# Moving the norms' transposes, and a row-wise Hadamard transform, from TensorE to GpSimd, VectorE and DRAM in an adaLN block

## The chip, the cores and the metric

The kernel runs on one core of a Trainium2 chip. The metric is the device time of one execution in microseconds; lower is better. The core has TensorE (PE in the profile; its weight loads are PEld), VectorE (DVE), ScalarE (ACT), GpSimd (POOL) and SyncE (SP), which here only issues transfers. TensorE writes to PSUM, which has eight banks in this kernel; everything else lives in SBUF, 128 partitions wide, or in DRAM.

## The reference, cut to what matters

The input x is 4 sequences of 1024 tokens by 512 channels, all in float32. Each sequence has its own modulation vectors, from which the norms' scales (ca, cb), shifts (sa, sb) and gates (ga, gb) come.

```python
h = layernorm(x) * (1 + ca) + sa
x = x + ga * attention(h)            # 16 query heads of 32, one shared key/value head, causal
h = layernorm(x) * (1 + cb) + sb
x = x + gb * ffn(h)

def ffn(h):
    x = fwht(h * SU_ug) / 64         # Hadamard transform over the 512 channels
    up, gate = (x @ W_up.T) * .., (x @ W_gate.T) * ..
    x = fwht(silu(gate) * up * SU_dp) / 64
    return (x @ W_down.T) * ..
```

What the change touches: the first norm's output h is needed with channels on the partitions (transposed), since the query, key and value products contract over channels. The second norm's output is needed transformed by fwht and transposed in the same way, since the up and gate products contract over channels too. The second fwht is not touched: it is folded into W_down at the start.

## The kernel before, in words

The 4096 tokens are worked off in eight blocks of 512 tokens, in the order `order` (sequence and half of the sequence: (0,0), (1,0), (0,1), (2,0), (1,1), (2,1), (3,0), (3,1)). A block has four tiles of 128 tokens, and two halves of 256 tokens. In the code `i` counts blocks from 0, `hh` counts halves over all blocks (0 to 15), `n` counts tiles over all blocks (0 to 31).

The work is written as streams (Python generators). Each stream yields operations (`Op`) with an engine, a planned cost, and the keys that it reads and writes. A planner (`Flow`) takes, again and again, the operation that can begin first by its planned times, with the streams' ranks to choose among those that begin within 0.3 us, and emits it. So the order of instructions on each engine, and of transfers on the SP queue, is fixed when the program is built; on the chip each engine works through its own order and waits wherever an input is late. All loads and stores of this change go through one queue, SP's (`load`, one issue line for all of them).

The streams that matter here:

- `first_norms`: for each half, loads two tiles (xn), takes statistics on VectorE (`stats_op`), the reciprocal root on GpSimd (`rstd_op`), normalizes on VectorE (`norm_op`), turns the half by eight TensorE transposes of 128x128 into two PSUM banks (`turned`, L315), and ScalarE applies scale and shift on the way into hT (`modulate`, L324).
- `fronts`: the key/value and query products from hT (L289). hT is a single buffer of one half, so the next half's hT waits for these products.
- `scores`, `minima`, `exps`, `reciprocals`, `scales`, `turns`, `attend`, `finish`: attention for each tile of 128 queries, ending in the output projection (L289, `ow`) and the multiplication by the gate on VectorE (L644).
- `add`: reloads the tile of x (xr, two slots), adds the output bias and the attention's result on GpSimd (L659, L661), stores the sum, and normalizes it (statistics L294, rstd L300 and L301, L305).
- `second_norms`: for each half, eight transposes (L315), ScalarE modulation into u2 (L324), one butterfly over pairs of 128-channel chunks on GpSimd (VectorE in the first block) into v4 (L689, L692), four Hadamard products by a 128x128 matrix (L700), a copy on ScalarE (L705) and two butterfly steps on VectorE (L708) into bt. Then four differences (L712) prepare Strassen-like sums of the activations. bt holds one block, so bt is refilled only after the block before has finished its gate and up products (`st.gated`).
- `gate_up`: the gate and up products by a seven-product scheme (L982) with 16 steps of 128 hidden channels per block; weights wg (two slots) and wu (three slots) are loaded per step, and GpSimd forms sums of them (`mixes`, L946). Partial results are summed on VectorE (L1069) and copied by ScalarE (L1056, L1060); `multiply` applies silu (L1085 to L1095).
- `down`: W_down products (L1120): 16 steps for the first half of the block (beside the gating) and 16 for the second half (after it), with one load of wd (three slots) per step.
- `outputs`: multiplies by the gate gb (L1149), adds x on GpSimd (L1154), and stores.

`gate_up` and `down` have the lowest ranks: TensorE does attention and norms first and fills up with feed-forward work.

Of the kernel before, what the change touches and what calls it, by code (L numbers as in the profile page):

```python
# [19 lines left out]
P = 128  # L20
# [3 lines left out]
NT = TB // P  # L24
# [136 lines left out]
def adaln_block(ctx, tc, x_d, small_d, const_d, wmod_d, qwT_d, kwT_d, vwT_d, vb_d, owT_d, ob_d,  # L161
# [5 lines left out]
    dram = ctx.enter_context(tc.tile_pool(name="dram", bufs=1, space=DRAM))  # L167
    psum = ctx.enter_context(tc.tile_pool(name="psum", bufs=1, space=PSUM))
    flow, banks = Flow(), Banks()
    ps = psum.tile([P, 8, 512], F32, name="ps")  # L170

    def sb(name, *shape):
# [1 line left out]

    x2_d = dram.tile([B * S, D], F32, name="x2_d")
    wd_d = dram.tile([NFC, P, D], F32, name="wd_d")
    gates_d = dram.tile([3, B, D], F32, name="gates_d")
    rows = [slice(HD * j, HD * j + HD) for j in range(4)]


# [51 lines left out]
    ga, obga, y = sb("ga", D), sb("obga", D), sb("y", D)  # L232

    u2, v4 = sb("u2", 2, HB), sb("v4", NDC, HB)

    make_identity(nc, ident)
    nc.gpsimd.memset(mhalf, -0.5)
# [66 lines left out]
    def norm_op(x, xk, m, rs, rkey):  # L304
        return Op("DVE", 0.62, lambda: nc.vector.tensor_scalar(x, x, m, rs, ALU.subtract, ALU.mult), [rkey], [xk])  # L305

    def turned(x, xk, done=None):

        yield banks.have(2)
        bb = banks.take(2)  # L310

        def turns():
            for dc in range(NDC):
                for j in range(2):
                    nc.tensor.transpose(ps[:, bb[dc // 2], (dc % 2) * HB + j * P:][:, 0:P],  # L315
                                        x[:, j, dc * P:(dc + 1) * P], ident)
        yield Op("PE", 8 * 0.107 + 0.05, turns, [(xk, 0), (xk, 1)], [bk(b) for b in bb], mode="full")
        found.append(bb)
# [10 lines left out]
    def first_norms(halves):  # L329
        for hh in halves:  # L330
            i, hf = divmod(hh, 2)
            b = order[i][0]

            x, xk = (xo, "xo") if hh == 1 else (xn, "xn")
            yield lambda: st.fronts >= (hh - 1 if hh > 1 else 0)
            for j in range(2):
                r = token(2 * hh + j)
                yield load(0.25, x[:, j, :], x_d[r:r + P, :], [(xk, j)])
            m = mv["a"][:, hf]
            for j in range(2):  # L340
                yield stats_op("a", j, x[:, j, :], m[:, j, :], [(xk, j)], ("mva", hf, j))
            rs = rstd["a"][:, hf, :]
            yield rstd_op(rs, m[:, :, 1], [("mva", hf, 0), ("mva", hf, 1)], ("rstda", hf))
            for j in range(2):
                yield norm_op(x[:, j, :], (xk, j), m[:, j, 0:1], rs[:, j:j + 1], ("rstda", hf))
            yield lambda: st.fronts >= hh
            yield from turned(x, xk)
            bb = found.popleft()
            for dc in range(NDC):
                yield modulate(hT[:, dc, :], bb, dc, modT[:, 1, dc, b:b + 1], modT[:, 0, dc, b:b + 1],  # L350
                               ["mod0", "mod1"], [("hT", dc // 2 * 2)])
                if dc % 2:
                    banks.give(bb[dc // 2])
            st.first_normed = hh + 1
# [294 lines left out]
    def add():  # L649

        for i in range(NBLK):
            if new_batch(i):
                yield load(0.25, obga, gates_d[2, order[i][0], :].partition_broadcast(P), ["obga"], [("gates", 2)])
            for ql in range(NT):
                j, n = ql % 2, i * NT + ql
                x, xk, r = xr[:, j, :], ("xr", j), n * P
                yield lambda: st.turned > n - 2
                yield load(0.25, x, x_d[token(n):token(n) + P, :], [xk])
                yield Op("POOL", 1.3, lambda: nc.gpsimd.tensor_add(x, x, obga), ["obga"], [xk])  # L659
                yield lambda: bool(to_add)  # L660
                yield Op("POOL", 1.3, lambda: nc.gpsimd.tensor_add(x, x, y), ["y"], [xk])  # L661
                to_add.popleft()
                st.y_held = False
                yield load(0.25, x2_d[r:r + P, :], x, [("x2", n)], [xk])
                m, rs = mv["f"][:, j, :], rstd["f"][:, j, 0:1]
                yield stats_op("f", n, x, m, [xk], ("mvf", j))
                yield rstd_op(rs, m[:, 1:2], [("mvf", j)], ("rstdf", j))
                yield norm_op(x, xk, m[:, 0:1], rs, ("rstdf", j))
                st.added = n + 1

    def second_norms():


        for i in range(NBLK):
            b = order[i][0]
            for hf in range(2):
                n0 = i * NT + 2 * hf
                yield lambda: st.added >= n0 + 2
                yield from turned(xr, "xr")
                bb = found.popleft()  # L680
                st.turned = n0 + 2
                for c in (0, 2):
                    for dc in (c, c + 1):
                        yield modulate(u2[:, dc - c, :], bb, dc, sc2[:, dc, b:b + 1], bi2[:, dc, b:b + 1],
                                       ["mod4"], ["u2"])
                    banks.give(bb[c // 2])
                    for e, dc in (("add", c), ("sub", c + 1)):
                        if i:
                            yield Op("POOL", 0.66, lambda: getattr(nc.gpsimd, "tensor_" + e)(  # L689
                                v4[:, dc, :], u2[:, 0, :], u2[:, 1, :]), ["u2"], [("v4", dc)])  # L690
                        else:
                            yield Op("DVE", 0.4, lambda: getattr(nc.vector, "tensor_" + e)(  # L692
                                v4[:, dc, :], u2[:, 0, :], u2[:, 1, :]), ["u2"], [("v4", dc)])
                yield lambda: st.gated >= i
                yield banks.have(2)
                bb = banks.take(2)

                def products():
                    for dc in range(NDC):
                        nc.tensor.matmul(ps[:, bb[dc // 2], (dc % 2) * HB:][:, 0:HB], had, v4[:, dc, :],  # L700
                                         start=True, stop=True)
                yield Op("PE", mm(HB, 4), products, [("v4", dc) for dc in range(NDC)] + ["had"],
                         [bk(b) for b in bb], mode="full")
                w2 = u2.rearrange("p a n -> p (a n)")
                yield Op("ACT", act_cost(512), lambda: nc.scalar.copy(w2, ps[:, bb[1], :]), [bk(bb[1])], ["u2"])  # L705
                banks.give(bb[1])
                for e, k in (("add", hf), ("sub", 2 + hf)):
                    yield Op("DVE", 0.7, lambda: getattr(nc.vector, "tensor_" + e)(  # L708
                        bt[:, k].rearrange("p a n -> p (a n)"), ps[:, bb[0], :], w2), [bk(bb[0]), "u2"], [("bt", k)])
                banks.give(bb[0])  # L710
            for o, u, w in ((T1, B12, B11), (T2, B22, T1), (T3, B22, B12), (T4, B21, T2)):
                yield Op("DVE", 0.7, lambda: nc.vector.tensor_sub(bt[:, o], bt[:, u], bt[:, w]),  # L712
                         [("bt", u), ("bt", w)], [("bt", o)])
            st.normed = i + 1
# [60 lines left out]
    def mods():  # L775
        for _ in range(6):
# [42 lines left out]
            if part == 4:  # L819
# [5 lines left out]
                        nc.vector.tensor_scalar_mul(sc2[:, dc, :], modT[:, 3, dc, :], sus[:, dc:dc + 1])  # L825
                        nc.vector.tensor_scalar_mul(bi2[:, dc, :], modT[:, 2, dc, :], sus[:, dc:dc + 1])
                yield Op("DVE", 1.0, scales, ["mod3"], ["mod4"])
            if part in (2, 5):
                for g in ((0, 2), (), (), (1,))[part - 2]:
                    v = gt[:, g, 2]  # L830
                    yield banks.have(1)
                    o, = banks.take(1)

                    def turn_back():
                        for dc in range(NDC):
                            nc.tensor.matmul(ps[0:B, o, dc * P:(dc + 1) * P], v[:, dc, :], ident, start=True, stop=True)
# [322 lines left out]
    def early(rank, later):  # L1159
# [1 line left out]

    ranked = [
        (0, copies), (0, sums), (0.5, multiply), (1, outputs), (0.2, load_weights_once), (2, load_jobs), (2, mods),
        (early(1.8, 3), attend), (early(1.8, 3), finish), (early(1.8, 3), add), (early(2.2, 4), minima), (early(2.05, 4), scores), (early(1.7, 5), second_norms), (0, lambda: first_norms([0])), (0.1, lambda: first_norms([1])), (2.1, lambda: fronts([0])),
        (6.1, lambda: first_norms(range(2, NHALF))),
        (6, lambda: fronts(range(1, NBLK))), (early(2.3, 7), turns), (early(2.5, 8), exps), (1.5, reciprocals), (early(2.4, 7.5), scales), (2.6, butterflies),
        (2.15, transforms), (0.3, mixes), (9, hand_over), (10, lambda: load_gu("wu", 3, wupT_d)), (10, lambda: load_gu("wg", 2, wgT_d)), (10, load_wd),
# [54 lines left out]
```

## Time and profile before

| what | value |
|---|---|
| median of 3 runs | 2108.74 us (2106.20 to 2109.54) |
| profiled execution | 2106.39 us, its span 2104.6 us |
| granted TensorE clock, mean | 0.992 |
| TensorE busy | 2029.8 us |
| VectorE busy | 1325.7 us |
| ScalarE busy | 1174.0 us |
| GpSimd busy | 663.4 us |
| transposes of the norms (L315) | 256 instructions |
| Hadamard products of the second norm (L700) | 128 instructions |
| DMA engines busy, queue of SP | 31.4% |

How to read the profile: a line of the cost groups names the source line, the engine, the operation, output and input tiles, their shapes and the count; then, after the bar, busy time in us and the mean of one in ns; then the engine's idle time just before these instructions and what ended it. The chain of work that ended last is followed back from the last instruction; its pieces show what set the time. A float32 product counts as two TensorE instructions, a transpose as one. A transfer's "us to landing" runs from its issue to the arrival of its data.

### The profile page before, as it was taken

How to read it: one execution, taken by the hardware profiler on the slowest of the kernel's cores; microseconds unless marked ns; L12 is line 12 of the kernel's file. 1: busy time of each engine (PE TensorE's matmuls, PEld its weight loads, DVE VectorE, ACT ScalarE, POOL GpSimd, SP SyncE). 2: the span in 40 equal slices, each digit the busy share in tenths (PEclk: the TensorE clock that was granted, in tenths of full speed). 3: DMA queues.
4: the chain of work that ended last, by engine and by line, in shares of the span. 5: the costliest groups of instructions: out<-in, count | busy, mean ns of one | idle time of the engine just before them, and what ended most of it. 6: DMA issues, size and time to landing. Idle time of an engine off the chain costs nothing.

```text
span 2104.6 us, 41766 instructions
## 1 busy us (share of the span) xinstructions
PE 2029.8 (96%) x16408; PEld 1306.5 (62%) x16408; DVE 1325.7 (63%) x3085; ACT 1174.0 (56%) x2497; POOL 663.4 (32%) x814
## 2 busy tenths in 40 slices
PE   6989999999999999999999999999999999999998
PEld 4457666566656666646667476665666646675774
DVE  3975657776864657576874676784755878542441
ACT  3856746665744756465663676567744667431220
POOL 2572342223331242323331133231432223232331
PEclk9889999999999999999999999999999999999999
DMA  6144222432233322342221432232322233225333
GB/s 207 57 131 131 81 86 76 121 106 72 76 91 91 116 85 72 86 136 86 81 76 57 132 90 85 62 91 86 110 76 66 71 112 91 78 86 148 110 101 115
DMA packets 222075, 201.54 MB, mean 96 GB/s; under 512 B 14252, under 2 KB 161836, under 8 KB 221880
## 3 DMA queue, kind: packets, MB, share of 16 engines
q1 hardware_dynamic: 217944, 196.45, 31.4%
q8 instruction: 129, 2.11, 0.4%
q10 hardware_dynamic: 3936, 2.43, 0.4%
q14 instruction: 66, 0.54, 0.1%
HBM read 177.84 MB, written 21.00 MB: 94 GB/s over the span
## 4 chain that ended last, share of the span: by engine, by line
PE 89%; DVE 5%; issue 2%; DMA 1%; POOL 1%; ACT 1%; SPq 0%; ACTq 0%; POOLq 0%; DVEq 0%
PE ps L982 37%; PE ps L1120 20%; PE ps L289 12%; PE ps L591 9%; PE ps L467 7%; DVE p L563 2%; PE ps L627 2%; DVE p L491 1%; PE ps L315 1%; PE ps L700 1%; DMA raw<-in_wmod 1%; DVE g L1095 1%; DVE s L1069 0%; POOL p L545 0%; PE ps L890 0%
## 5 line engine op out<-in xcount | busy, mean ns | idle before, releaser
L1120 PE MATMUL ps<-wd,g 128*128 128x512 f32 x1024 | 479.7, 603 | 14.1 <-DVE g L1095 11.3
L514 ACT ACTIVATE p<-p,nm 128x512 f32<-128x512 f32 (+7 forms) x512 | 391.3, 768 | 29.0 <-DVE nm L491 28.8
L982 PE MATMUL ps<-bt,ws 128*128 128x256 f32 x1536 | 376.5, 381 | 1.3 <-ACT s L1056 1.3
L548 ACT ACTIVATE p<-p,rden 128x640 f32<-128x640 f32 (+7 forms) x480 | 349.7, 784 | 42.9 <-DVE rden L528 42.2
L1069 DVE TENSOR_TENSOR s<-ps,s 128x256 f32<-128x256 f32 x384 | 160.2, 420 | 330.4 <-PE ps L982 250.8
L563 DVE STREAM_TRANSPOSE p<-p 128x512 f32<-128x512 f32 (+7 forms) x256 | 340.8, 1358 | 27.7 <-ACT p L548 24.5
L1120 PEld LDWEIGHTS ps<-wd,g 128*128 128x128 f32 x1024 | 185.0, 189 | 232.8 <-issue 180.0
L982 PEld LDWEIGHTS ps<-bt,ws 128*128 128x128 f32 x1536 | 288.9, 190 | 60.5 <-issue 13.4
L491 DVE CUSTOM_DVE_ANT_0 p<-ps,maskw 128x512 f32<-128x512 f32 (+3 forms) x512 | 276.9, 582 | 75.5 <-PE ps L467 75.0
L946 POOL TENSOR_TENSOR ws<-wu 128x256 f32<-128x256 f32 x128 | 105.3, 822 | 581.3 <-DMA wu<-in_wupT 556.9
L982 PE MATMUL ps<-bt,wu 128*128 128x256 f32 x1024 | 270.7, 387 | 0.5 <-DVE s L1069 0.5
L982 PE MATMUL ps<-bt,wg 128*128 128x256 f32 x1024 | 251.7, 382 | 1.3 <-DVE nm L491 0.6
L982 PEld LDWEIGHTS ps<-bt,wu 128*128 128x128 f32 x1024 | 187.7, 190 | 92.4 <-issue 53.4
L982 PEld LDWEIGHTS ps<-bt,wg 128*128 128x128 f32 x1024 | 192.0, 190 | 60.3 <-issue 26.2
L591 PE MATMUL ps<-p,vrep 32*32 32x256 f32 (+1 forms) x8256 | 198.1, 417 | 18.5 <-issue 9.2
L1085 ACT ACTIVATE th<-s,wgh 128x512 f32<-128x512 f32 x128 | 92.3, 721 | 182.3 <-DVE g L1095 122.5
L1060 ACT COPY s<-ps 128x256 f32<-128x256 f32 x128 | 47.5, 371 | 239.5 <-PE ps L982 238.9
L467 PE MATMUL ps<-kT,qT 32*128 32x512 f32 (+3 forms) x1536 | 178.7, 528 | 0.5 <-issue 0.2
L591 PEld LDWEIGHTS ps<-p,vrep 32*32 32x32 f32 x8256 | 121.4, 104 | 92.3 <-issue 35.3
L946 POOL TENSOR_TENSOR ws<-ws,wg 128x256 f32<-128x256 f32 x128 | 97.2, 760 | 173.6 <-DMA wg<-in_wgT 154.9
L604 ACT COPY oT<-ps 128x256 f32<-128x256 f32 x256 | 78.4, 383 | 126.7 <-PE ps L591 119.8
L491 DVE CUSTOM_DVE_ANT_0 p<-ps,maskw,nm 128x128 f32<-128x128 f32 (+3 forms) x256 | 127.9, 544 | 17.8 <-PE ps L467 17.6
(106 smaller groups left out, 2125.1 us busy)
## 6 DMA issues: line engine op xcount, KB each, us to landing
wd<-wd_d SPq DMA_DIRECT2D x256, 256.0 KB, 2.6
wu<-in_wupT SPq DMA_DIRECT2D x128, 256.0 KB, 2.8
wg<-in_wgT SPq DMA_DIRECT2D x128, 256.0 KB, 3.2
xr<-in_x SPq DMA_DIRECT2D x32, 256.0 KB, 3.1
x_d<-xr SPq DMA_DIRECT2D x32, 256.0 KB, 2.0
xo<-x_d SPq DMA_DIRECT2D x32, 256.0 KB, 3.9
out<-xo SPq DMA_DIRECT2D x32, 256.0 KB, 2.2
xn<-in_x SPq DMA_DIRECT2D x30, 256.0 KB, 3.3
```

The costliest lines, as they stand in the source:

```text
L289: nc.tensor.matmul(out, l, r, start=(k == 0), stop=(k == len(pairs) - 1))
L467: nc.tensor.matmul(ps[:, bb[j], m * n:(m + 1) * n], qT[r, c, u.ql * P:(u.ql + 1) * P], kT[r, u.kv[kb] * TB:u.kv[kb] * TB + n], start=True, ...
L491: yield Op("DVE", 0.245 + 0.00103 * n, lambda: nc.vector.tensor_tensor_reduce(o, ps[:, bb[j], k * n:(k + 1) * n], m, -1.0, nm[:, slot, 0, ...
L514: yield Op("ACT", act_cost(u.kmax) + 0.19, lambda: nc.scalar.activation(e, e, AF.Exp, bias=nm[:, slot, u.t, j:j + 1], scale=-1.0, accum_ou ...
L548: yield Op("ACT", act_cost(u.kmax), lambda: nc.scalar.activation(e, e, AF.Copy, scale=r), [("rden", ds, c)], [u.key(h)])
L563: yield Op("DVE", 0.135 + 0.00105 * 2 * u.kmax, lambda: nc.vector.transpose(e, e), [], [u.key(h), u.key(h + 1)])
L591: nc.tensor.matmul(ps[rows[c], bb[g], 0:w], vrep[rows[g], v0 + c, :], pv[rows[g], :, k:k + 32], start=(kt == 0), stop=(kt == nkt - 1))
L946: yield Op("POOL", 0.66, lambda: getattr(nc.gpsimd, "tensor_" + e)(a[o][0], a[x][0], a[y][0]), [a[n][1] for n in (x, y) if n != "A21" or o ...
L982: nc.tensor.matmul(o, w[:, c, :], bt[:, t, c, :], start=start and c == 0, stop=stop and c == 1, skip_group_check=True)
L1069: yield Op("DVE", 0.43, lambda: nc.vector.tensor_add(s[:, j, :], ps[:, bank, half * HB:(half + 1) * HB], s[:, j, :]), [bk(bank)], [sk[j]])
L1085: yield Op("ACT", act_cost(512), lambda: nc.scalar.activation(th, s[:, 0:2, :], AF.Tanh, scale=wgh[:, f:f + 1]), [sk[0], sk[1]], ["th"])
L1120: nc.tensor.matmul(ps[:, acc[j], :], g[:, j * P:(j + 1) * P], ff["wd"][:, m % NWD, :], start=(f == 0), stop=(f == NFC - 1))
```

## The change

Two constants, `ROWS, VIA_DRAM = 3, 4`, set from where the new way is used.

First norm, from half 4 (the third block) on: the normalized tile is transposed on VectorE, which turns each 32x32 square within the 128x512 tile in place. `turn` then stores the tile to DRAM (xT_d) with four transfers, one for each group of 32 partitions, which put the squares into their transposed places in runs of 32 elements (128 bytes). `turned_back` loads the transposed half from there into hT with two transfers, and ScalarE applies scale and shift in place in hT. The TensorE transposes of these halves and their PSUM banks go.

Second norm, from block 3 (the fourth) on: a new stream `transformed` applies scale and shift along the rows. Since channels now lie along the free axis, scale and shift are needed as rows, broadcast over the partitions; they are made at the start by two more turn-backs on TensorE, stored in gates_d, and loaded per sequence into v4's memory (sc2r, bi2r). VectorE does it in two scalar_tensor_tensor operations, which take the place of the normalization. GpSimd does the 512-point transform in nine steps, each an addition and a subtraction of even and odd elements (18 instructions of 128x256, back and forth between xr and ht, which lies in u2's memory). VectorE transposes the result, `turn` stores it, and `second_norms` loads it back into bt with two transfers per half. The transposes, the modulation, the butterflies and the Hadamard products of these blocks go; the four differences (L712) stay.

```diff
+    ROWS, VIA_DRAM = 3, 4
-    gates_d = dram.tile([3, B, D], F32, name="gates_d")
+    gates_d = dram.tile([5, B, D], F32, name="gates_d")
+    xT_d = {"a": dram.tile([NHALF, D, HB], F32, name="xTa_d"), "f": dram.tile([NHALF, D, HB], F32, name="xTf_d")}
...
+    ht = u2.rearrange("p a n -> p (a n)")
+    sc2r, bi2r = (v4[:, k:k + 2, :].rearrange("p a n -> p (a n)") for k in (0, 2))
...
+    def turn(which, n, x, xk):
+        hh, j = divmod(n, 2)
+        dst = xT_d[which][hh].rearrange("(b q) (j a i) -> j a q b i", q=32, j=2, a=4)[j]
+        for a, r in enumerate(rows):
+            yield load(0.0625, dst[a], x[r, :].rearrange("q (b i) -> q b i", i=32), [("xT", which, n, a)], [xk])
+
+    def turned_back(which, hh, c, dst, key):
+        return load(0.25, dst, xT_d[which][hh][c * P:(c + 2) * P, :].rearrange("(c p) n -> p c n", p=P), [key],
+                    [("xT", which, n, a) for n in (2 * hh, 2 * hh + 1) for a in range(4)])
...
@@ first_norms @@
+                if hh >= VIA_DRAM:
+                    yield Op("DVE", 0.67, lambda: nc.vector.transpose(x[:, j, :], x[:, j, :]), [], [(xk, j)])
+                    yield from turn("a", 2 * hh + j, x[:, j, :], (xk, j))
             yield lambda: st.fronts >= hh
+            if hh >= VIA_DRAM:
+                for c in (0, 2):
+                    yield turned_back("a", hh, c, hT[:, c:c + 2, :], ("hT", c))
+                for dc in range(NDC):
+                    yield Op("ACT", act_cost(HB), lambda: nc.scalar.activation(
+                        hT[:, dc, :], hT[:, dc, :], AF.Identity, bias=modT[:, 0, dc, b:b + 1],
+                        scale=modT[:, 1, dc, b:b + 1]), ["mod0", "mod1"], [("hT", dc // 2 * 2)])
+                st.first_normed = hh + 1
+                continue
...
@@ add @@
+                if i >= ROWS:
+                    to_fwht.append((n, m, rs))
+                    continue
...
+    def transformed():
+        for n in range(ROWS * NT, NBLK * NT):
...
+            yield lambda: bool(to_fwht)
+            _, m, rs = to_fwht.popleft()
+            yield Op("DVE", 0.7, lambda: nc.vector.scalar_tensor_tensor(x, x, m[:, 0:1], sc2r, ALU.subtract, ALU.mult),
+                     [("v4", 0), ("mvf", j)], [xk])
+            yield Op("DVE", 0.7, lambda: nc.vector.scalar_tensor_tensor(x, x, rs, bi2r, ALU.mult, ALU.add),
+                     [("v4", 2), ("rstdf", j)], [xk])
+            u, w = x, ht
+            for _ in range(9):
+                pairs = u.rearrange("p (n two) -> p two n", two=2)
+                for fn, h in (("add", 0), ("sub", D // 2)):
+                    yield Op("POOL", 0.66, lambda: getattr(nc.gpsimd, "tensor_" + fn)(
+                        w[:, h:h + D // 2], pairs[:, 0, :], pairs[:, 1, :]), [], [xk, "u2"])
+                u, w = w, u
+            yield Op("DVE", 0.67, lambda: nc.vector.transpose(x, ht), ["u2"], [xk])
+            yield from turn("f", n, x, xk)
+            st.added = st.turned = n + 1
...
@@ second_norms @@
+                if i >= ROWS:
+                    yield lambda: st.gated >= i
+                    for c in (0, 2):
+                        yield turned_back("f", 2 * i + hf, c, bt[:, c + hf], ("bt", c + hf))
+                    continue
...
@@ mods @@
-            if part in (2, 5):
-                for g in ((0, 2), (), (), (1,))[part - 2]:
-                    v = gt[:, g, 2]
+            if part in (2, 4, 5):
+                for g in ((0, 2), (), (3, 4), (1,))[part - 2]:
+                    v = gt[:, g, 2] if g < 3 else (sc2, bi2)[g - 3]
...
@@ ranked @@
-(early(1.8, 3), add), (early(2.2, 4), minima)
+(early(1.8, 3), add), (3.5, transformed), (early(2.2, 4), minima)
```

More of the change, by code (lines that the diff above doesn't have):

```diff
@@ L667, in add @@
                 yield rstd_op(rs, m[:, 1:2], [("mvf", j)], ("rstdf", j))
+                if i >= ROWS:
+                    to_fwht.append((n, m, rs))
+                    continue
                 yield norm_op(x, xk, m[:, 0:1], rs, ("rstdf", j))
                 st.added = n + 1
+    to_fwht = deque()
+    def transformed():
+        for n in range(ROWS * NT, NBLK * NT):
+            i, j = n // NT, n % 2
+            b = order[i][0]
+            x, xk = xr[:, j, :], ("xr", j)
+            if n == ROWS * NT or n % NT == 0 and new_batch(i):
+                yield lambda: st.normed >= ROWS
+                for k, (dst, c) in enumerate(((sc2r, 0), (bi2r, 2))):
+                    yield load(0.25, dst, gates_d[3 + k, b, :].partition_broadcast(P), [("v4", c), ("v4", c + 1)],
+                               [("gates", 3 + k)])
+            yield lambda: bool(to_fwht)
[14 more added lines that the diff above has]
+            st.added = st.turned = n + 1
     def second_norms():
@@ L1163, in adaln_block @@
         (0, copies), (0, sums), (0.5, multiply), (1, outputs), (0.2, load_weights_once), (2, load_jobs), (2, mods),
-        (early(1.8, 3), attend), (early(1.8, 3), finish), (early(1.8, 3), add), (early(2.2, 4), minima), (early(2.05, 4), scores), (early(1.7, 5), second_norms), (0, lambda: first_norms([0])), (0.1, lambda: first_norms([1])), (2.1, lambda: fronts([0])),
+        (early(1.8, 3), attend), (early(1.8, 3), finish), (early(1.8, 3), add), (3.5, transformed), (early(2.2, 4), minima), (early(2.05, 4), scores), (early(1.7, 5), second_norms), (0, lambda: first_norms([0])), (0.1, lambda: first_norms([1])), (2.1, lambda: fronts([0])),
         (6.1, lambda: first_norms(range(2, NHALF))),
```

## The prediction

> **What bounds the kernel now.** I read the busy shares first, then the chain of work that ended last, then the cost groups, then the chain's last 80 us in order of time, then the transfers.
>
> ```profile
> PE 2029.8 (96%) x16408; PEld 1306.5 (62%) x16408; DVE 1325.7 (63%) x3085; ACT 1174.0 (56%) x2497; POOL 663.4 (32%) x814
> PE 89%; DVE 5%; issue 2%; DMA 1%; POOL 1%; ACT 1%; SPq 0%; ACTq 0%; POOLq 0%; DVEq 0%
> ```
>
> TensorE is busy for 96% of the span and is 89% of the chain; it idles mostly at the start (20.5 and 10.5 us in the first two hundreds, 0 to 5 in each later one, 8.5 in the last). So a microsecond of matmul taken out after 200 us is worth a microsecond, unless TensorE then waits. GpSimd has two thirds of its time free, much of it at the head of its queue, waiting for weights.
>
> The pieces that the change removes, from the chain in order of time near the end (start, length, what):
>
> ```profile
> 1905.69 1.98 PE ps L1120 x4
> 1907.67 0.86 PE ps L982 x4
> 1908.53 1.73 PE ps L700 x8
> 1910.26 1.72 PE ps L1120 x4
> 1911.98 0.87 PE ps L315 x8
> 1912.85 6.87 PE ps L1120 x16
> 1919.72 1.73 PE ps L700 x8
> 1921.45 5.16 PE ps L1120 x12
> 1926.61 0.02 issue
> 1926.63 3.81 DMA wd<-wd_d
> ```
>
> A half block's eight transposes (L315) take 0.87 us and its Hadamard products (L700) 1.73 us, end to end with their neighbours: nothing hides them. The last line matters too: where TensorE runs down products (L1120) alone, the wd loads are almost late already.
>
> Prices for what is added, from the cost groups (the third split by shape):
>
> ```profile
> L689 POOL TENSOR_TENSOR v<-u 128x256 f32<-128x256 f32 x56 | 40.2, 737 | 54.7 <-ACT u L324 54.7
> L661 POOL TENSOR_TENSOR xr<-xr,y 128x512 f32<-128x512 f32 x32 | 42.8, 1338 | 278.8 <-DVE y L644 258.6 <-DVE rden L528 19.9
> L563 DVE STREAM_TRANSPOSE p<-p 128x512 f32<-128x512 f32 x32 | 20.7, 685 | 4.0 <-ACT p L548 3.9
> L1087 DVE SCALAR_TENSOR_TENSOR th<-th,s 128x512 f32<-128x512 f32 x128 | 93.5, 730 | 43.3 <-ACT th L1085 42.9
> x_d<-xr SPq DMA_DIRECT2D x32, 256.0 KB, 2.0
> xr<-in_x SPq DMA_DIRECT2D x32, 256.0 KB, 3.1
> ```
>
> A 256-wide GpSimd add takes 0.74 us; a 512-wide VectorE transpose 0.69. The last two lines end with the time to landing.
>
> Small packets, from the transfers between 15 and 20 us, then between 25 and 30:
>
> ```profile
> DMA packets 1644, 1.16 MB, mean 231 GB/s; under 512 B 1143, under 2 KB 1143, under 8 KB 1644
> q10 hardware_dynamic: 1127, 0.13, 18.1%
> ...
> DMA packets 2039, 1.13 MB, mean 225 GB/s; under 512 B 16, under 2 KB 1980, under 8 KB 2039
> q1 hardware_dynamic: 2039, 1.13, 92.1%
> ```
>
> Sixteen engines have 80 us in 5 us. In the first window 1127 packets (mean 115 B, mostly the 128 B rows of the vwT loads) took 18.1% of that, 12.8 ns each; in the second 2039, nearly all of 512 B, 92.1%, 36 ns each.
>
> **The change, part by part.** The order of the changed program on each engine shows what moves.
>
> *TensorE.* Gone: the transposes of 12 first-norm halves (5th on) and of 10 second-norm halves (blocks four to eight), 22 x 0.87 = 19.1 us; Hadamard products of 10 halves, 17.3. Added: two more turn-backs of 8 instructions (L836: 24 take 3.1 us), 2.1 us. Net -34.3, nearly all after 200 us.
>
> *GpSimd.* Gone: 40 adds (29.5 us). Added: 20 tiles x 18 adds of 128x256 whose inputs take every second element. No row shows a stride of two on GpSimd: low end 0.74 (L689, same output size), high end 1.34 (L661, if a strided 256 costs the 512 it spans). I take 0.74, the row of the same element count: 360 x 0.74 = 266 us; busy rises to about 900 us, 43%. This is off TensorE's path, but a tile's chain becomes 18 x 0.74 = 13.3 us where before it had two to four adds.
> The Trainium skill (GPSIMD Engine Reference, section on performance pitfalls) puts a cliff of 50% at reads that step by more than 8 bytes. These step by exactly 8, the near side; on the far side the tile would take 13.3 x 1.5 = 20 us, between my ends. No run here shows it.
>
> *VectorE.* Gone: 20 normalizations (L305, 0.65) and 20 adds (L708, 0.68), 26.6 us. Added: 40 scalar_tensor_tensor x 0.73 and 44 transposes x 0.69, 59.6. Net +33 us on 1326. *ScalarE.* 40 modulations (0.56) and 10 copies (0.58) go, -28 us; the first norm's modulations stay, reading SBUF. Neither bounds: busiest hundreds 77% and 76%.
>
> *Transfers.* 44 tiles leave in 4 stores of 512 packets of 128 B: 90,112 packets. The trace has no such store. Between 12.8 ns (reads of that size) and 36 ns (512 B) a tile occupies the engines for 1.6 to 4.6 us, in all 3.4 to 9.6% of the span; 512 B stores land like 512 B loads (wd_d 5.7, raw 5.6 us), so I take 20 ns, nearer to the size, and no stall of its own. With the 44 loads back and 8 broadcasts this adds 230 issues on SP at 0.37 us, 85 us, in the one queue that also issues wg, wu and wd.
> The Trainium skill (DMA: Bandwidth & Descriptors, specifications) says transfers under 512 B are read-modify-write. The reads above contradict a penalty for loads only, so it stays as a rival.
>
> *Waits, first kind: late normalized input.* In the new order, gating of the last block starts after the last output-projection product and just 32 down instructions: 16 x 1.72 = 27.5 us of cover. The last tile needs meanwhile: y 0.69, add 1.34, statistics 0.86, rstd 0.84, scaling 0.73, transform 13.3, transpose 0.69, store issue 1.5, landing 2.0, load issue and landing 3.5, first difference 0.7: 26.2, with ten hand-overs of about 0.08 us 27. Before, the stretch from that product to rstd took 7.1 us (1874.45 to 1881.56) against 3.7 by this sum, so up to 3.4 of queueing: 27 to 30.4. Moreover the turn stands on SP ahead of the last three wd loads of that pass: issued at 20.5 to 24, the next lands 2.9 later at 23.4 to 27, and its product is due at 22.4. TensorE loses 1 to 5 us; I take 3. Block six has the same place (28 us of product work from its last tile to gating): 3 more. In the other blocks at least ten down steps stand between the load back and gating.
>
> *Second kind: wd behind turns.* In a second pass of down, three slots release a load two steps ahead, 3.4 us, of which issue and landing (0.34 and 2.6) use 2.9. SP has about fourteen groups of turns or turned-back loads inside these passes, each 0.7 to 1.5 us of issue; each costs 0 to 1 us, the low end where attention products lie between. Of 0 to 14 I take 6.
>
> *Third kind: hT.* It is now refilled by a load (0.4 and 3.1, the second 0.4 later) and four modulations, partly beside it, 5.7 us in all, after the product that frees it. The order leaves 4.3, 5.5, 6.7 and 6.9 us of product work at the tightest places, 10 or more elsewhere: 0 to 4, take 2.
>
> *Fourth:* busier VectorE and GpSimd queues delay gate sums and weight mixes. TensorE waited 27 us in weight loads for L1095; a tenth to a third more: 3 to 9, take 5. That GpSimd's transform delays the mixes I cost at nothing: before, L946 waited 557 us for wu, and a mix ends some 5 us before its product; from 5 us late on it would count.
>
> Sum: -34.3 + 6 + 6 + 2 + 5 = -15.3. The profiled execution took 2106.4 us (span 2104.6 and 1.8 around it), which gives 2091.1; the median of the runs lies 2.3 above it, so I say **2093**.
>
> **The rivals.**
> 1. *All of it hides.* The four waits nearly vanish: 2108.7 - 34.3 + 0 to 8, 2074 to 2082. For it: TensorE had almost no wait in 1800 us. Against: the 27.5 us of cover at the end is counted.
> 2. *The SP queue eats the gain.* Each wait at its upper end, 10 + 14 + 4 + 9 = 37: 2111, no change. For it: SP already waits in order (218 us for GpSimd's xr).
> 3. *Slower: the strided adds cost up to 1.34 us.* A tile then takes 24 us, 10.8 more. At the two tight boundaries that is 22 us; at the other 18 tiles the turn's lateness passes to the weight loads behind it, 5 us of it hidden by the slots: up to 5.8 x 18 = 104, half of it likely. 2093 + 22 + 52 = 2167; 2115 with the boundaries alone. It decides against the change from about 1.05 us per add. The trace has no such read.
> 4. *Slower: small stores are dear.* At 72 ns (twice a 512 B packet) a tile blocks the rings for 9.2 us, and weight loads queue behind it, 4 us beyond their slots in perhaps half of 44 tiles: 2093 + 90 = 2183. This is what the Trainium skill's 512 B rule would do; the 12.8 ns reads speak against it.
>
> **How the numbers follow.** Forecast (2083 to 2104) 0.50; rival 1, 0.17; rival 2, 0.13; rival 3, 0.13; rival 4, 0.07. About 0.2% (4 us) is what a measurement of this kernel can tell from no change. Faster: 0.50 + 0.17 and 0.01 of rival 2, 0.68; same, 0.10 of rival 2; slower, the rest, 0.22. The range leaves out the upper parts of rivals 3 and 4: 2072 to 2126.
>
> **What would show it.** Right: near 80 transposes (L315 before) and 48 Hadamard products (L700 before), TensorE still 96% busy; the transform's adds near 0.74 us; GpSimd near 900 us; turn stores landing in 2 to 3 us; a wait of some us before gating in the last and the sixth block. Wrong: adds above 1 us, TensorE's share falling below 95% with waits on wd or on GpSimd's ws, or wd landing well above 2.6 us.

## The result, and the profile after

| | before | changed |
|---|---|---|
| median, runs alternating on one chip | 2107.47 us (2102.92 to 2109.54) | 2075.81 us (2072.41 to 2078.02) |
| profiled execution / its span | 2106.39 / 2104.6 us | 2072.41 / 2070.6 us |
| TensorE busy / idle in the span | 2029.8 / 74.8 us | 1992.2 / 78.4 us |

The ratio is 0.9851 [0.9829, 0.9873]: 31.7 us less in the median, 34.0 in the profiled span. The forecast was 2093, a gain of 15.7 on the 2108.7 it started from. The direction held, and the time lies inside the range, but the gain is twice the one forecast, and the time is that of the first rival (2074 to 2082, all waits hide).

Two lines of the page of the changed kernel, and the row of the SP queue (packets, MB, share of 16 engines):

```profile
PE 1992.2 (96%) x16168; PEld 1272.1 (61%) x16168; DVE 1361.6 (66%) x3131; ACT 1150.5 (56%) x2447; POOL 863.1 (42%) x1134
...
q1 hardware_dynamic: 324008, 221.65, 37.3%
...
PE 86%; DVE 5%; DMA 3%; issue 2%; POOL 2%; SPq 1%; ACT 0%; ACTq 0%; POOLq 0%; DVEq 0%
```

TensorE has 37.6 us less to do and still is busy for 96% of a shorter span; it idles 3.6 us more than before. The forecast had -34.3 and +19 for the same two things. GpSimd ends at 863 us, below the 900 forecast, and that gap is in the two rows of the adds. The added work in the cost groups of the changed kernel, split by shape (busy us, mean ns after the bar):

```profile
L731 POOL TENSOR_TENSOR u<-xr 128x256 f32<-128x256 f32 x200 | 124.4, 638 | 19.2 <-DVE xr L725 13.4
L731 POOL TENSOR_TENSOR xr<-u 128x256 f32<-128x256 f32 x160 | 98.6, 634 | 5.6
L734 DVE STREAM_TRANSPOSE xr<-u 128x512 f32<-128x512 f32 x20 | 14.1, 706 | 25.6 <-POOL u L731 25.6
L725 DVE SCALAR_TENSOR_TENSOR xr<-xr,rstdf,v 128x512 f32<-128x512 f32 x20 | 18.4, 922 | 2.7 <-POOL rstdf L309 1.5
L723 DVE SCALAR_TENSOR_TENSOR xr<-xr,mvf,v 128x512 f32<-128x512 f32 x20 | 16.1, 805 | 11.5 <-DMA x_d<-xr 9.6 <-DVE nm L524 0.9 <-DMA xr<-in_x 0.8
```

The strided add takes 0.64 us, below both ends that the prediction gave it (0.74 and 1.34): the two rows sum to 223 us where 266 were forecast. The two scalar_tensor_tensor take 0.81 and 0.92, not 0.73. The idle time behind L734's bar is time in which VectorE stood still for GpSimd's transform: 25.6 us in 20 tiles, 11.4 of them in the last tile, where little else is left for VectorE to do.

The stores and loads of the turn (KB each, us from issue to landing):

```profile
xTa_d<-xn SPq DMA_DIRECT2D x96, 64.0 KB, 2.3
hT<-xTa_d SPq DMA_DIRECT2D x24, 256.0 KB, 3.2
xTf_d<-xr SPq DMA_DIRECT2D x80, 64.0 KB, 2.1
bt<-xTf_d SPq DMA_DIRECT2D x20, 256.0 KB, 6.4
```

Stores of 64 KB in runs of 128 B land in 2.1 to 2.3 us; the 256 KB stores of whole rows take 2.0 (x_d) and 2.4 us (out). The DMA engines were busy for 31.4% of 16 x 2104.6 us before and 37.3% of 16 x 2070.6 after: 1784 us more for 106,064 more packets, or 17 ns a packet; if all of it is put down to the 90,112 of these stores, 20 ns. The prediction took 20. The run with every store twice, below, gives a lower price.

What TensorE waited for in the changed kernel (us in total, times, longest):

```profile
PE ps L1192 <- DVE g L1167: 9.1, 15, 0.9
...
PE ps L1054 <- DVE rden L561: 4.6, 1, 4.6
...
PE ps L1192 <- DMA wd<-wd_d: 2.7, 5, 0.7
```

The first row had 11.3 us before, the third 1.9. No row of TensorE names hT, and the weight mixes (ws, L1018) ended one wait, of 0.8 us, in the first 200 us. After that the second row is the only wait above 2 us, and it is the sixth block's (block index 5).

### The profile page after: what moved, and what is told of

It reads as the page before. It is cut to its first block, busy times and chain, and to the rows that moved or that the text cites. A ratio compares the mean times of both kernels' runs of the same rounds, so it can differ in the third digit from the quotient of the medians.

```text
span 2070.6 us, 41956 instructions
## 1 busy us (share of the span) xinstructions
PE 1992.2 (96%) x16168; PEld 1272.1 (61%) x16168; DVE 1361.6 (66%) x3131; ACT 1150.5 (56%) x2447; POOL 863.1 (42%) x1134
## 3 DMA queue, kind: packets, MB, share of 16 engines
q1 hardware_dynamic: 324008, 221.65, 37.3%
## 4 chain that ended last, share of the span: by engine, by line
PE 86%; DVE 5%; DMA 3%; issue 2%; POOL 2%; SPq 1%; ACT 0%; ACTq 0%; POOLq 0%; DVEq 0%
PE ps L1054 36%; PE ps L1192 19%; PE ps L297 11%; PE ps L624 9%; PE ps L500 7%; PE ps L660 2%; DVE p L596 1%; DVE p L524 1%; POOL u L731 1%; DMA raw<-in_wmod 1%; PE ps L962 1%; POOL xr L731 1%; DVE g L1167 1%; SPq L286 1%; PE ps L965 1%
## 5 line engine op out<-in xcount | busy, mean ns | idle before, releaser
L1018 POOL TENSOR_TENSOR ws<-wu 128x256 f32<-128x256 f32 x128 | 103.8, 811 | 476.6 <-DMA wu<-in_wupT 461.5
L1054 PEld LDWEIGHTS ps<-bt,wg 128*128 128x128 f32 x1024 | 193.3, 191 | 59.6 <-issue 30.6
L624 PE MATMUL ps<-p,vrep 32*32 32x256 f32 (+1 forms) x8256 | 196.5, 415 | 20.4 <-issue 11.4
L1018 POOL TENSOR_TENSOR ws<-ws,wg 128x256 f32<-128x256 f32 x128 | 101.0, 789 | 114.8 <-DMA wg<-in_wgT 93.7
L694 POOL TENSOR_TENSOR xr<-xr,y 128x512 f32<-128x512 f32 x32 | 43.0, 1344 | 242.2 <-DVE y L677 238.6
```

Of the source, the lines that this page charges most:

```text
L624: nc.tensor.matmul(ps[rows[c], bb[g], 0:w], vrep[rows[g], v0 + c, :], pv[rows[g], :, k:k + 32], start=(kt == 0), stop=(kt == nkt - 1))
L1054: nc.tensor.matmul(o, w[:, c, :], bt[:, t, c, :], start=start and c == 0, stop=stop and c == 1, skip_group_check=True)
```

## The experiments

Where the expectations name theories by a letter, A says in short that other work covers the forecast's waits, so that what leaves TensorE is gained; B, in the first four, that the waits are there at about the sizes of the forecast. C was formed on the way: what is lost depends on how the order, fixed when the program is built, meets the real durations, and this order meets them well. Each experiment edits the changed kernel; its ratio is to the kernel before on the same chip. Differences to the changed kernel are of medians, unless the text says that they are of ratios.

**Only the first norm's way**

```diff
-    ROWS, VIA_DRAM = 3, 4
+    ROWS, VIA_DRAM = 8, 4
```

> Only the first norm turned through VectorE and DRAM; the second norm stays on TensorE (the two added turn-backs at the start stay too). Theory A, all added work is covered and the gain is the TensorE work taken out: -10.4 + 2.1 = -8.3 us, about 2099. Rival B, the waits of the prediction are there at the sizes given (stores and loads ahead of wd, hT refilled late, busier queues, together some 7 us for this half of the change) and the gain came from elsewhere: -1, about 2106.

2101.36 us beside 2106.36 of the kernel before: 0.9978 [0.9966, 0.9990]. TensorE's busy time falls by 8.7 us (12 halves at 0.87 are 10.4), its idle time by 0.2. But that is the profile of the fastest of ten runs (2097.48 to 2104.66); the gain of the medians is 5.0 us, between the two expectations, so whether all of the removed work is gained stays open. TensorE idles 6.0 us from 1400 to 1500 us here too, most of it at the start of the sixth block's gating, though the second norm is as before.

**Only the second norm's way**

```diff
-    ROWS, VIA_DRAM = 3, 4
+    ROWS, VIA_DRAM = 3, 16
```

> Only the second norm by rows on GpSimd and turned through DRAM; the first norm stays on TensorE. Theory A: -8.7 - 17.3 + 2.1 = -23.9, plus 2 to 5 us at the end, where the cover is short: 2084 to 2089. Rival B: with 6 us at the two tight boundaries and 6 of late wd loads and busy queues: -12, about 2095.

2100.14 us: 0.9972 [0.9955, 0.9989]. By the forecast's prices TensorE loses 10 x 0.87 + 17.3 - 2.1 = 23.9 us of work; 6.2 of it came out, and the time lies above both expectations. The stretch from 1400 to 1500 us, around the sixth block's gating, in this kernel (length, busy time of PE, PEld, DVE, ACT, POOL with counts, granted clock, DMA share, GB/s), and what TensorE, and VectorE before it, waited for there:

```profile
1400.00:1500.00 100.00, 87.78 (x954) 51.71 (x953) 65.16 (x184) 73.55 (x203) 45.53 (x68) 0.93 0.31 88
```

```profile
PE ps L1054 <- DVE bt L784: 8.9, 1, 8.9
...
DVE xr L723 <- DMA v<-gates_d: 2.9, 1, 2.9
DVE xr L725 <- DMA v<-gates_d: 1.4, 1, 1.4
```

12.2 us idle in these 100, and a lower clock; the same stretch of the kernel before has 0.6 us idle at clock 1.00. The last two rows are waits that the prediction did not have: the scale and shift rows of the next sequence (v, two loads of 256 KB) come late, and VectorE stands before them while the sixth block's differences (L784) wait behind in its queue. The two halves alone give 5.0 and 6.2 us, and both in one kernel 31.7: the parts do not add, so a cost per part cannot be the whole account.

**Each add twice, order unchanged**

```diff
-                    yield Op("POOL", 0.66, lambda: getattr(nc.gpsimd, "tensor_" + fn)(
-                        w[:, h:h + D // 2], pairs[:, 0, :], pairs[:, 1, :]), [], [xk, "u2"])
+                    def emit():
+                        for _ in range(2):
+                            getattr(nc.gpsimd, "tensor_" + fn)(w[:, h:h + D // 2], pairs[:, 0, :], pairs[:, 1, :])
+                    yield Op("POOL", 0.66, emit, [], [xk, "u2"])
```

> Each of the 18 additions of a tile's transform is issued twice (the same result again), in the same planned order on every engine, so that each tile's turn is ready some 11 us later (18 x 0.61 as the profile of the changed kernel has them). Theory A, the plan keeps so much other work between a turn and its use that TensorE feels it only where the cover is short: 11 us at the last block, 0 to 11 at the sixth, nothing in the 18 other tiles: 2087 to 2098. Rival B, a late turn holds up the weight loads behind it on the SP queue in every block (the working of rival 3): 22 us at the boundaries and about 50 elsewhere: near 2150.

2316.16 us: 1.0998 [1.0970, 1.1026], 240 us above the changed kernel, for 223 us more of GpSimd. Both theories fell (2087 to 2098, and 2150). VectorE's wait for the transform, and what TensorE then waited for (the edit moves later lines by two):

```profile
DVE xr L736 <- POOL u L733: 248.3, 20, 23.8
```

```profile
PE ps L1056 <- DVE s L1143: 61.1, 7, 11.6
PE ps L500 <- DVE nm L524: 34.1, 5, 9.5
PE ps L624 <- DVE p L596: 33.6, 9, 13.2
PE ps L1194 <- DMA wd<-wd_d: 23.0, 5, 13.2
```

This is the wait that the prediction's section on added waits left out. The transpose (L734, here L736) stands on VectorE's queue until GpSimd's eighteen adds are done, and behind it stand gate sums, attention's minima and attention's transposes, which TensorE needs within a few us. The wait grew from 25.6 to 248.3 us, and the rows above are its victims. GpSimd, with more than half of its time free, became a bound only because another engine's queue waits in order for it.

**Each add twice, and the planner told**

The edit before this one stands too; only the planned cost is changed against it.

```diff
-                    yield Op("POOL", 0.66, emit, [], [xk, "u2"])
+                    yield Op("POOL", 1.32, emit, [], [xk, "u2"])
```

> The same doubled additions as before, but the planner is told: 1.32 us for a doubled addition instead of 0.66, so it puts VectorE's transpose, the stores and everything around them that much later and other work ahead. Theory C, what costs time is an instruction that is late against the plan, because it holds up what stands behind it on VectorE's and SP's queues; the amount of GpSimd work costs little: 2076 plus 11 to 30 us at the two short covers, 2087 to 2106. Rival D, the longer chain per tile is itself the bound, however it is planned: near 2316 again.

2124.48 us: 1.0089 [1.0069, 1.0110]. In this kernel:

```profile
DVE xr L736 <- POOL u L733: 34.9, 15, 4.9
```

The same instructions, the order planned for their real length: 192 of the 240 us are gone. So most of the 240 us was lateness against the plan, and not GpSimd's work. 49 us over the changed kernel remain, more than the 11 to 30 that theory C allowed; why the slower transform costs that much when it is planned for was not followed further.

**Adds of contiguous halves, order unchanged**

```diff
-                pairs = u.rearrange("p (n two) -> p two n", two=2)
+                pairs = u.rearrange("p (two n) -> p two n", two=2)
```

It computes another transform than the one asked for, with the same number and size of instructions.

> Each addition and subtraction of the transform reads the two contiguous halves of the row in place of its even and odd elements; the plan and the order are the same, the transform's result is another one. If a contiguous addition takes 0.73 us, as the weight sums do, against 0.61 for the strided ones, a tile's transform becomes 2.1 us longer, 1.2 us beyond its planned length. Theory C: 20 tiles late by 1.2 us, 0 to 25 us more than the changed kernel, 2076 to 2100. By the slope of the doubled additions from the first microsecond on (240 us for 220 us of GpSimd work): 47 us more, 2123. If contiguous additions take 0.61 too, 2076, and the weight sums' 0.73 has another cause (two tiles in place of one).

That contiguous operands are dearer was not known before. In this kernel:

```profile
L731 POOL TENSOR_TENSOR u<-xr 128x256 f32<-128x256 f32 x200 | 148.1, 757 | 18.0 <-DVE xr L725 12.2
L731 POOL TENSOR_TENSOR xr<-u 128x256 f32<-128x256 f32 x160 | 118.0, 755 | 5.6
L734 DVE STREAM_TRANSPOSE xr<-u 128x512 f32<-128x512 f32 x20 | 14.2, 711 | 52.9 <-POOL u L731 52.9
```

0.756 us instead of 0.636, which happens to be the price in the forecast (0.74, from an add of contiguous operands). With it the kernel takes 2095.81 us, 0.9956 [0.9943, 0.9969], 20.0 above the changed kernel (22 by the ratios) and 2.8 above the forecast. So 0.12 us per add, 2.2 us per tile, is worth 20 us here. VectorE's wait behind L734's bar doubles to 52.9 us, TensorE idles 12.5 us more than in the changed kernel, and is busy 5.9 longer at a clock of 0.991 instead of 0.993. The loss is spread over the blocks from 1200 us on, with 3.7 us of idle time more from 1400 to 1500.

**Every store of the turn twice, the second to a spare tile**

```diff
...
+            op = load(0.0625, dst[a], x[r, :].rearrange("q (b i) -> q b i", i=32), [("xT", which, n, a)], [xk])
+            def emit(first=op.emit, a=a, r=r):
+                first()
+                nc.sync.dma_start(spare[a], x[r, :].rearrange("q (b i) -> q b i", i=32))
+            op.emit = emit
+            yield op
...
```

> Each turn's four stores are issued a second time, into a DRAM tile that nobody reads, right beside the first: 176 more stores of 512 packets of 128 bytes on the SP queue, in the same planned order. Theory A, SP and the DMA engines have room at these places: 0 to 4 us more than the changed kernel, 2076 to 2080. Rival B, stores ahead of wd cost 0 to 1 us a group as summed in the prediction: 6 to 14 us more, 2082 to 2090.

2106.38 us: 1.0003 [0.9988, 1.0018], 30.6 above the changed kernel for 176 more stores, 0.17 us each, and above both expectations. The stores still land in about 2 us. The SP queue's share of the DMA engines is 40.0% of 16 x 2104.0 us, 1108 us more than in the changed kernel for 90,112 more packets of 128 B: 12 ns a packet. In this kernel (lines moved by six):

```profile
PE ps L1198 <- DMA wd<-wd_d: 8.1, 6, 2.9
PE ps L1060 <- DVE rden L567: 7.4, 1, 7.4
```

The wd loads behind the stores on SP's queue are later (8.1 us for 2.7), and the sixth block's gating is too. So the second rival's mechanism is real, and at the changed kernel's number of issues it costs little (2.7 us of waits). These two rows explain 8 of the 17 us that TensorE idles more; whether the issues on SP or the packets cost the rest was not separated.

**The last block's second norm back on TensorE**

```diff
-                if i >= ROWS:
+                if ROWS <= i < NBLK - 1:
...
-        for n in range(ROWS * NT, NBLK * NT):
+        for n in range(ROWS * NT, (NBLK - 1) * NT):
...
```

> The last block's second norm goes back to TensorE, ScalarE and VectorE; blocks four to seven stay by rows. TensorE work returns, 2 x 2.6 = 5.2 us, and the wait before the last block's gating (some 3 us in the changed kernel's profile) goes: 2 us more, 2078, if the short cover at the end costs only what TensorE idles; up to 3 us less, 2073, if the idle time there also costs clock.

2077.07 us: 0.9862 [0.9846, 0.9879], the same as the changed kernel within the intervals. In its profile TensorE is busy 8.6 us longer and idles 3.2 less over the whole span. Whether the last block gains by the new way, the intervals do not tell.

**The same work in another planned order**

```diff
-                    yield Op("POOL", 0.66, lambda: getattr(nc.gpsimd, "tensor_" + fn)(
+                    yield Op("POOL", 0.61, lambda: getattr(nc.gpsimd, "tensor_" + fn)(
```

> Only the planner's cost of an addition changes, from 0.66 to 0.61 us, what it takes on the chip; the work is the same, the order another. Theory C, lateness against the plan costs time: nothing is early any more, a tile's transform has no margin (before 18 x 0.05 = 0.9 us, 0.026 in the mean more by queueing), so 0 to 15 us more than the changed kernel, 2076 to 2091. Theory A, only the work counts: 2076.

> Only the planner's cost of an addition changes, from 0.66 to 0.75 us, above what it takes on the chip. Theory C: a tile is ready 2.5 us before its plan, nothing is late, but each tile's turn is planned 1.6 us later than in the changed kernel and the two short covers lose that: 2072 to 2080. If the changed kernel's place between its neighbours is chance of the plan, this one may land up to 15 us above it.

The second has 0.75 in that place. Only the planner's cost differs, so every instruction is the same and the order of some is not. With 0.61: 2096.72 us, 0.9931 [0.9908, 0.9955]. With 0.75: 2101.42, 0.9957 [0.9940, 0.9973]. By the ratios they are 17 and 22 us above the changed kernel; above what was expected, though 0.61 is as near to the measured mean of 0.636 as the 0.66 of the changed kernel. The instructions are the same, but TensorE is busy for 2001.3 and 2005.5 us instead of 1992.2, at lower granted clocks (0.989 and 0.987 instead of 0.993); the rest of the loss is idle time. The stretch from 1400 to 1500 us with 0.75, and a wait of TensorE in it:

```profile
1400.00:1500.00 100.00, 81.92 (x937) 43.64 (x936) 67.12 (x199) 69.33 (x191) 41.49 (x62) 0.90 0.35 93
```

```profile
PE ps L624 <- DVE p L596: 8.1, 1, 8.1
```

18 us idle at clock 0.90, here before an attention product whose transpose on VectorE was late. With 0.61 (the profile is of the fastest of four runs, 2088.25 us) that stretch has 7.8 us idle at clock 0.95, against 6.1 at 0.97 in the changed kernel; more of the loss lies from 1900 to 2000 us, 6.2 us idle at clock 0.95 against 1.2 at 1.00.

**The new ways from a block, or a half, earlier**

```diff
-    ROWS, VIA_DRAM = 3, 4
+    ROWS, VIA_DRAM = 2, 2
```

> Row-wise second norm already from the third block, and the first norm's turn through DRAM from the second block on. TensorE work taken out: another 2 x 2.6 for the second norm and 2 x 0.87 for the first, 6.9 us. Theory A or C, the added work is planned in and covered: 2069. Rival B, a new plan brings its own late places, as the plans of the two halves did: 2075 to 2085.

> Row-wise second norm already from the third block; the first norm as in the changed kernel (from the third block). TensorE work taken out: 5.2 us. With no late place of its own: 2071. The variant that moved both a block earlier lost 27 us between 1400 and 1500 us; if the row-wise part brought that, this one is near 2110 too, if the first norm's part, near 2071.

The second has `2, 4`. More work taken off TensorE, and slower: 2116.95 us, 1.0054 [1.0039, 1.0069], and 2118.04 us, 1.0043 [1.0028, 1.0058]. The stretch of 1400 to 1500 us again, in the kernel with `2, 2`:

```profile
1400.00:1500.00 100.00, 73.24 (x912) 41.56 (x902) 67.39 (x191) 65.39 (x177) 37.17 (x55) 0.89 0.31 88
```

26.8 us idle; with `2, 4` 19.2. Since both lose alike, the loss comes with the second norm's row-wise part, not with the first norm's. But each of these kernels also has another order, and another order alone cost 17 and 22 us above, so how much is the row-wise part's own is not shown. None of the edits came out faster than the changed kernel.

## Why the prediction was right and wrong, point by point

*TensorE, -34.3.* Right: its busy time fell by 37.6. Where the 3.3 beyond come from is open.

*The last block's chain, +3.* Right in mechanism, and an upper end in size. The chain of work that ended last in the changed kernel, around the last tile (start, length, what):

```profile
1879.65 0.70 DVE y L677
...
1880.42 1.28 POOL xr L694
1881.71 3.03 DMA x_d<-xr
...
1884.87 0.76 DVE xr L723
...
1885.72 0.76 DVE xr L725
...
1886.55 1.19 POOL u L731 x2
...
1897.85 0.72 DVE xr L734
...
1900.63 2.81 DMA wd<-wd_d
...
1903.48 5.42 PE ps L1192 x12
1908.90 1.73 PE ps L1054 x8
```

And the first differences, in VectorE's timeline:

```profile
1907.01 2.10 DVE L784 TENSOR_TENSOR bt<-bt 128x512 f32<-128x512 f32 x3 [8.45 <-DMA bt<-xTf_d]
```

From the last output-projection product (end 1879.53) to the end of the first of these three differences 28.2 us pass, between the 27 and 30.4 that were worked out. Gating began 1.2 us later, at 1908.90, so TensorE did not wait for the data; the wd load stuck behind the four store issues is there. TensorE is busy for 30.1 of the 32 us from 1880 to 1912, so it loses 1.9: 0.47 is the wait for that wd load, 0.58 one for an earlier wd load, and 0.78 a pause between the first gating products. Two parts of the working were off and nearly cancel: scaling in place waits 3.03 us for the store of the sum that still reads xr, where 1.7 us of statistics had been counted, and the transform takes 11.3 us instead of 13.3.

*Block six, +3.* The place was right; the reason was right only in part. The gating products there, in TensorE's timeline of the changed kernel:

```profile
1456.99 1.13 PE L1054 MATMUL ps<-bt,wg 128*128 128x256 f32 x4
1462.70 2.00 PE L1054 MATMUL ps<-bt,ws 128*128 128x256 f32 x4 [4.58 <-DVE rden L561]
1465.43 3.75 PE L1054 MATMUL ps<-bt,ws 128*128 128x256 f32 x8 [0.72 <-ACT s L1128]
```

And VectorE's timeline just before:

```profile
1456.52 0.75 DVE L723 SCALAR_TENSOR_TENSOR xr<-xr,mvf,v 128x512 f32<-128x512 f32 x1 [2.41 <-DMA x_d<-xr]
1457.19 0.68 DVE L1221 TENSOR_TENSOR y<-ps,gb 128x512 f32<-128x512 f32 x1
...
1461.80 0.76 DVE L784 TENSOR_TENSOR bt<-bt 128x512 f32<-128x512 f32 x1
```

The turned-back load of this half on SP's queue, its time to landing (two loads), and the share that the queue had of the DMA engines from 1454 to 1459 us:

```profile
1452.23 0.91 SPq L286 DMA_DIRECT2D bt<-xTf_d  x2
...
DMA to landing us min/median/max: 6.9/7.1/7.2
...
q1 hardware_dynamic: 1204, 1.73, 93.7%
```

The waiting products need the differences of L784, and the first difference needs the first of these loads. TensorE ran out of work at 1458.12. The load landed no sooner than 1459.1, 6.9 us after its issue where the forecast counted 3.5 for issue and landing: the queue kept the DMA engines nearly full, with the next sequence's scale and shift rows, a store and other loads issued beside it. So the normalized data was late, by 1 us. Then the difference stood until 1461.80 in VectorE's queue, behind L723 of a later tile, which had waited 2.41 us for the store that still read xr, and behind attention's work. That is the larger part, 2.7 us, and the forecast did not have it. The stall costs more than its length: the four matmul instructions after it take 2.00 us and the next eight 3.75, where four take 1.03 and eight 1.97 elsewhere. With 6.1 us idle and a clock of 0.97 in this stretch, the cost is above the 3 taken.

*wd behind turns, +6.* Measured +0.8 (2.7 us of waits, 1.9 before). With the stores doubled the same waits are 8.1 us.

*hT, +2.* None. *Busier queues, +5.* None in the rows that the forecast went by: the row named, weight loads waiting for the gates' product, fell from 27.0 to 25.8 us, and TensorE's own wait for it from 11.3 to 9.1.

*Prices.* VectorE's scalar_tensor_tensor was 0.08 to 0.19 us dearer than its row; the four stores of a tile issue in 1.9 us where 1.5 was counted; small packets cost 12 ns by the doubled stores, below the 20 taken. What each of these is worth alone was not measured. The Trainium skill (GPSIMD Engine Reference, section 7) has reads that step by no more than 8 bytes on the cheap side of its 50% cliff; the 0.636 us of the adds that step by 8 agrees.

*The step that failed* is the sum of the four waits, +19 to -34.3, of which TensorE's idle time shows 3.6. By term: wd behind turns was put at 6 and cost 0.8, the busier queues at 5 and hT at 2 and cost nothing that the rows show; only the late input, put at 6, came, and it came mostly in the sixth block. The removed work was therefore gained almost whole. One price was mis-sized too, the add at 0.74 for 0.636 us. In the forecast's sum it enters only the late input, through the tile's chain of 13.3 us. In the kernel it reaches further: at a measured 0.756 in the same order the time is 2095.81, which is near the forecast's. That agrees in the sum, not in the places: the waits at the larger price lie mostly in VectorE's queue, which the forecast priced only as "busier". For the same reason the third rival was too mild: it let adds decide from about 1.05 us, at 2115 and more. Doubled adds (1.26 us) gave 2316 in this order; between 0.636 and 0.756 us, 20 us were lost, and a straight line through them would have used up the whole gain at about 0.83.

But the price is not all of it. With the real adds and another order the time was 17 and 22 us higher. So a forecast near 2093 was about right for the two orders tried beside this one, and that this order does better is, as far as the runs show, luck. What makes one order good stays open: most that lose do so between 1400 and 1500 us, where attention of a later block, the turn and the sixth block's gating share VectorE's queue, but not all, and no run shows a feature of the order from which the loss could be told ahead. One suspect was left untested. In this stretch the next sequence's scale and shift rows are loaded (v<-gates_d), just ahead of the sixth block's turned-back load, and VectorE stands before them or before the transfers beside them: 2.4 us in the changed kernel, 2.9 and 1.4 with only the second norm's way. No run loads these rows earlier. They are not the whole story: with the planned cost of 0.75 TensorE's wait of 8.1 us began before they were issued.

## What to carry to other kernels

When work moves to an idle engine, look for the first instruction on a busy, in-order queue that waits for it, and price what stands behind that instruction; the mover's own busy time says little. In a program with a fixed order, the same longer instruction costs far more when the plan does not know of it (240 us against 49 here), so measure a new form of instruction before planning with it. And where two orders of the same work differ by 20 us, a part-by-part sum can't be trusted below that.

## What the runs showed of the hardware that was not expected

- On GpSimd, adding even and odd elements of one 512-wide float32 tile takes 0.636 us, adding its two contiguous halves 0.756.
- A stall of TensorE slows the products after it. After 4.58 us without work four matmul instructions took 2.00 us instead of 1.03, and the granted clock was 0.50 for 6.8 us; after 0.78 us eight took their usual 1.97. With adds twice the mean granted clock fell to 0.945, and the same products cost 61 us more of busy time than in the changed kernel. The Trainium skill (TensorE: Matmul & The Clock Gate, "Why this matters for your kernels") asks for no gap above about 3 us; these two cases agree. But shorter stalls slowed as well: 1.86 us (planned cost 0.75, ending at 1118.5) and 2.32 us (stores twice, ending at 1167.8) were each followed by 3.4 us at clock 0.50, while 2.04 us in the kernel before (ending at 1808.2) was not.
- 90,112 packets of 128 B, stored to DRAM, cost at most 20 ns of an engine each in the changed kernel, 90,112 more cost 12 ns each, and a turn's stores land in 2.1 to 2.3 us. The dear packet of the fourth rival (72 ns) is not seen at this size.
